# Earlier bank returns, a shift on GpSimd, split token loads and a reordered list in the first layer of a cross-attention kernel

## The chip, the cores and the metric

The kernel runs on one core of a Trainium2 chip. Its time is the device time in microseconds of one execution, given as the median of several runs. Everything is in fp32. The core has five engines, each with its own queue of instructions, taken in order: TensorE (PE in the profile, its weight loads PEld), VectorE (DVE), ScalarE (ACT), GpSimd (POOL) and SyncE (SP, which here only issues DMAs). Matmul results land in PSUM, eight banks of 128 partitions by 512 fp32 values. SBUF holds everything else.

## The reference, cut to what matters

Two layers on 2048 tokens of width 256, with a context of 1601 rows of width 192.

```python
# first layer: tokens route over the context and a gated unit takes the result
tok    = context @ W_proj + b_proj                      # 1601 x 256
attn   = softmax(x @ tok.T / 16)                        # 2048 x 1601
routed = attn @ tok
ps_n, in_n = ln(x, g_state, beta_state), ln(routed, g_input, beta_input)
u = sigmoid([ps_n, in_n] @ W_u + b_u)
r = sigmoid([ps_n, in_n] @ W_r + b_r)
cand = tanh([r * ps_n, in_n] @ W_n + b_n)
x = ln((1 - u) * x + u * cand, g_out, beta_out)
# second layer: 16 heads of 16
h = ln(x, ln1); x = x + mha(h, h, sa_*)
h = ln(x, ln2); x = x + mha(h, context, ca_*)
h = ln(x, ln3); x = x + gelu(h @ mlp_w1.T + mlp_b1) @ mlp_w2.T + mlp_b2
```

The kernel never forms `tok` for the context. It multiplies the tokens by W_proj's transpose first (`queries`), takes scores against the raw context, averages the raw context with the softmax weights (`mean_context`), and projects that mean (`project`).

## The kernel before, in words

Tokens are cut into 16 tiles of 128 (index t) and four blocks of 512 (index b). The program traces operations one after another. A helper `kept` pins an operation behind the one traced before it on the same engine, so that for all compute the engine's order is the traced order. DMAs are not pinned; the framework places them in a queue by its own estimate. The framework sets every semaphore from the order of accesses to each tile.

**First layer, attention** (up to about 206 us). PSUM is a pool, `halves`, of four tiles of two banks, handed out in turn; a tile is given again when all work on its last use is done.
- SyncE issues the loads in traced order: W_proj, the first 512 tokens transposed (`load_xT(0)`, L113 to L115), the context (L121, L123), then bias rows, tokens and further transposed tokens (L224 to L230).
- `queries(b)` (L253) multiplies a block of transposed tokens by the weights, in place in `xy_sb`; ScalarE copies both banks back (L265).
- `query_bias(t)` (L276): GpSimd multiplies a tile of tokens with b_proj (L279) and ScalarE sums it into `cbs`.
- `scores(t)` (L282): TensorE takes scores of a tile against 1601 context rows in two passes (128 features, then 64) into two `half` tiles. VectorE takes the two maxima (L302), and then two operations on one column, on VectorE as well, make the shift (L306 to L310): the smaller of the two negated maxima less the bias, then plus the bias and over 16. ScalarE takes two exponentials with that shift (L313), which frees the two tiles. `turned(t)` (L320) is VectorE's 32x32 block transpose of the result.
- `turn_context` and `spread_context` lay the context out in 32-row pieces by TensorE transposes and 20 DMAs.
- `mean_context(h)` (L361), for each half h of the tokens: four `half` tiles at once; a first pass fills the first bank of each (128 features), a second pass the second bank (64 features). Then eight evictions (L388), c = 0 four times, then c = 1, ScalarE for six and VectorE for two, into `xy_sb`.
- `project(t4)` (L397): four tiles of tokens into one `half`. `project_end(t4)` (L406): for each of the four, VectorE scales by the softmax denominator and adds b_proj out of PSUM into `routed` (L410), then takes the mean and variance (`norm_stats`, L170 and L171).
- `begin_in(b)` (L421) takes the inverse roots of four tiles' variances: two small VectorE operations each, then twelve GpSimd operations on 4 columns (L185 to L188), once for `routed` and once for x, and a VectorE operation that waits for the first. `normed_tile` normalizes x on VectorE, `routed_tile` normalizes `routed` on ScalarE.

The first token half runs `mean_context(0)` and then scores of tiles 8 to 15; after these come `project` 0 and 1, their `project_end` with `begin_in`, `mean_context(1)`, `project` 2 and 3 and their `project_end`. Then `halves` is closed, and a pool `ps_all` of eight one-bank tiles (`bank`) takes its place.

**The list FIRST** (about 206 to 400 us). One list of names, written out by hand (L1093 on), sets the order of the gated unit and of the second layer's preparation. A name calls a step with its arguments: `bi` begin_in, `nx` normed_x (four tiles), `nr` normed_r (four tiles on ScalarE), `ti` a turn of four tiles of normalized x or routed by TensorE with a ScalarE eviction, `r` a reset gate (TensorE, ScalarE's sigmoid, VectorE's product into `rp_T`), `u` and `c` update gate and candidate (TensorE, VectorE's bias add, ScalarE's function), `b` the blend and its statistics (VectorE), `ro` and `rs` inverse roots (GpSimd), `no` and `ns` normalizations, `ts` turns for self attention, `k`, `v`, `q`, `qs` keys, values, queries and their spreading by SyncE's DMAs (L576), `ck`, `cv`, `cs` the same for cross attention (`cs` issues from ScalarE's queue), `REL` gives first-layer memory back and starts the second context load, `cw` loads cross attention's weights, and `L` is one lead unit: four score matmuls and four VectorE maxima (L660), work that the main loop would otherwise do. There are 19 of them. Around the list's start, the second layer's buffers are made: 16 DMAs by SyncE (`ones_beside`, L545), eight DMAs that load `sa_wo` (`load_wo`, L527, issued by GpSimd), eight for `bias8` (L564) and three rows of zeros for the query buffers (L642).

**The main loop** (400 us to the end) goes over 464 units of scores, exponentials and values, less 19 done ahead, with the projections and norms hung in between; then the MLP. The change doesn't touch it.

Of the kernel before, what the change touches and what calls it, by code (L numbers as in the profile page):

```python
# [10 lines left out]
ALU = mybir.AluOpType  # L11
# [3 lines left out]
P = 128  # L15
S = 2048
D = 256
L = 1601
# [3 lines left out]
HD = 16  # L22
HP = 32
# [4 lines left out]
QB = 512  # L28
# [42 lines left out]
def xattn_kernel(  # L71
# [9 lines left out]
    nc = tc.nc  # L81
# [11 lines left out]
    def kept(ins):  # L93
        tc.keep_in_program_order(ins)
        return ins
# [14 lines left out]

    xy_sb = pa.tile([P, 2, S], F32, name="xy_sb")

    def load_xT(b):  # L113
        at_b = slice(b * QB, (b + 1) * QB)
# [86 lines left out]
    T8 = NT // 2  # L201
# [32 lines left out]
    def half():  # L234
        return halves.tile([P, 2, QB], F32, name="half")
# [14 lines left out]
    kept(nc.scalar.copy(wT_sb[:, :, P:], pt[:, :, P : 2 * P]))  # L250


    def queries(b):  # L253
        pt = half()
        for m in range(2):
            for c in range(2):
                mm(
                    pt[:, m, :],
                    wT_sb[:, c, m * P : (m + 1) * P],
                    xy_sb[:, c, b * QB : (b + 1) * QB],  # L260
                    start=(c == 0),
                    stop=(c == 1),
                )
        for m in range(2):
            kept(nc.scalar.copy(xy_sb[:, m, b * QB : (b + 1) * QB], pt[:, m, :]))  # L265

# [94 lines left out]
    def mean_context(h):  # L361


        accs = [half() for _ in range(4)]

        def part(dst, i, kb, feats, **kw):
            r = slice(i * HP, (i + 1) * HP)
            mm(
                dst[:, : T8 * HP].rearrange("p (t a) -> p t a", a=HP),
                ctx4[r, kb, feats],  # L370
                pT[r, :, kb * HP : (kb + 1) * HP],
                skip_group_check=True,
                **kw,
            )

        for kb in range(KB):
            for i, acc in enumerate(accs):
                part(acc[:, 0, :], i, kb, slice(0, P), start=(kb == 0), stop=(kb == KB - 1))
        for kb in range(KB):
# [3 lines left out]
        uT = xy_sb[:, :, h * T8 * P : (h + 1) * T8 * P].rearrange("p c (t i a) -> p c t i a", i=4, a=HP)  # L383
        for c in range(2):
            for i, acc in enumerate(accs):
                copy = nc.vector.tensor_copy if (i % 2 and c) else nc.scalar.copy
                kept(
                    copy(  # L388
                        uT[:, c, :, i, :],
                        acc[:, c, : T8 * HP].rearrange("p (t a) -> p t a", a=HP),  # L390
                    )
                )
        ts = slice(h * T8, (h + 1) * T8)
        kept(nc.vector.tensor_add(rdens[:, ts], dens[:, ts, 0], dens[:, ts, 1]))
        kept(nc.vector.reciprocal(rdens[:, ts], rdens[:, ts]))
# [7 lines left out]
                mm(pt[:, i, :], xy_sb[:, c, tok], w, start=(c == 0), stop=(c == 1))  # L403
        return pt

    def project_end(t4, pt):  # L406
        for i in range(4):
            t = 4 * t4 + i
            kept(
                nc.vector.scalar_tensor_tensor(  # L410
                    routed[:, t, :], pt[:, i, :], rdens[:, t : t + 1], row("b_proj"),
                    ALU.mult, ALU.add,
                )
            )
            norm_stats(mv_r, routed[:, t, :], t)

# [31 lines left out]
    xns.update({2: xns[0], 3: xns[1]})  # L448


    queries(0)
    query_bias(0)
    scores(0)
    turn_context(0, 4)
# [50 lines left out]
    for t4, pt in got:  # L505
        project_end(t4, pt)
    l0.close()


# [7 lines left out]
    def heads(ap, w):  # L517
        return ap.rearrange("p (h w) -> p h w", w=w)

    def load_wo(pool, w, name):  # L520

        t = pool.tile([P, G // 2, D], F32, name=name)
        v = w.rearrange("(pr hf j w) n -> hf j w pr n", hf=2, j=4, w=HP)
        for hf in range(2):
            for j in range(4):
                r = j * HP + hf * HD
                nc.gpsimd.dma_start(t[r : r + HD, :, :], v[hf, j, :HD])  # L527
        return t

    ps_all = ctx.enter_context(tc.tile_pool(name="ps_all", bufs=8, space=PSUM))  # L530
# [369 lines left out]
    def normed_x(b):  # L900
        for i in range(4):
            normed_tile(xns[b][i], 4 * b + i)

    def normed_r(b):
        for t in range(4 * b, 4 * b + 4):
            routed_tile(t)
# [143 lines left out]
    ca = {}  # L1050
# [14 lines left out]
    def load_ca_weights():  # L1065
        wqs["ca"] = load_compact(
            ca["pool"], ca_wq, P, "ca_wq_sb", nc.gpsimd, ca["stage"].tile([P, 4 * D], F32, name="stage")
        )
        wos["ca"] = load_wo(ca["pool"], ca_wo, "ca_wo_sb")

    def k_ca_block(pr, n):
        n0, nw = even_blocks(L, 4)[n]
# [2 lines left out]
    def k_ca_spread(pr):  # L1075
# [6 lines left out]


    STEPS = {
        "bi": begin_in, "nx": normed_x, "nr": normed_r, "ti": turned_in, "r": reset, "u": update,
        "c": candidate, "b": blend, "ro": root_out, "no": normed_out, "rs": root_sa,
        "ns": normed_sa, "ts": turned_sa, "k": k_sa_block,
        "v": lambda b, i: v_block("sa", sa_wv_sb, hT_sa, 4 * b + i),
# [2 lines left out]
        "cs": k_ca_spread, "cv": lambda i: v_block("ca", ca_wv_sb, ca["ctx"], i), "L": lead_unit,  # L1091
    }
    FIRST = (  # L1093
# [9 lines left out]
    ).split()  # L1103
    for w in FIRST:
        name = w.rstrip("0123456789.")
# [157 lines left out]
```

## Time and profile before

| what | us |
| --- | --- |
| median of three runs | 1945.0 (1943.71 to 1945.75) |
| the profiled execution | 1942.26 |
| its span | 1940.5 |
| TensorE busy | 1908.6 |
| VectorE busy | 1430.3 |
| ScalarE busy | 1334.4 |
| GpSimd busy | 671.8 |
| granted TensorE clock, mean | 0.993 |
| last first-layer token tile evicted from PSUM (L410) | 205.95 |
| end of the list FIRST | about 400 |

The profile is of one execution; its own time is beside its span, and 2.7 us under the median. An engine's busy time counts its instructions and not its waits. In a row of the timeline the first two numbers are the start and the length, `x` is how many instructions were merged, and the brackets tell how long the engine stood before it and what ended that. `SPq` and `ACTq` are the issuing of DMAs.

### The profile page before, as it was taken

Reading aid. Unit: us, or ns where it says so; the run is one execution under the profiler, and the core shown is the slowest. Engines: PE = TensorE matmul, PEld = TensorE weight load, DVE = VectorE, ACT = ScalarE, POOL = GpSimd, SP = SyncE. Lnnn points to the kernel's source line nnn. Section 1 sums busy time; section 2 is a strip of 40 time slices with the busy share of each in tenths; the row PEclk is TensorE's granted clock in tenths of the full one; section 3 lists DMA queues with packets and bytes.
Section 4 is the critical chain, followed back from the end, with each engine's and each line's share of the span. In section 5 each row is a group of like instructions: output and inputs, shape, how many; then the busy total and the mean of one; then the engine's idle time right before and its main releaser. Section 6 shows DMA issues by size and latency. Waiting matters only on the chain.

```text
span 1940.5 us, 39176 instructions
## 1 busy us (share of the span) xinstructions
PE 1908.6 (98%) x14774; PEld 852.7 (44%) x14774; DVE 1430.3 (74%) x2554; ACT 1334.4 (69%) x2590; POOL 671.8 (35%) x850
## 2 busy tenths in 40 slices
PE   9997999999999999999999999999999999999999
PEld 4756675533333333433333334333333433443366
DVE  4472476788888888888888888788888878886210
ACT  3230423268887888788878887887888788888621
POOL 1201424124443444344444444343544343443010
PEclk9998998999999999999999999999999999999999
DMA  8310403600000000000000000000000000000000
GB/s 212 99 33 2 51 1 70 81 12 5 5 5 5 5 5 5 5 5 8 5 5 5 5 5 5 5 5 4 26 27 5 7 6 5 5 5 2 1 22 22
DMA packets 32766, 38.27 MB, mean 20 GB/s; under 512 B 12416, under 2 KB 24832, under 8 KB 32192
## 3 DMA queue, kind: packets, MB, share of 16 engines
q1 hardware_dynamic: 30496, 29.72, 7.3%
q0 software_dynamic: 1424, 4.38, 0.8%
q10 hardware_dynamic: 656, 1.67, 0.6%
q8 instruction: 116, 1.90, 0.4%
q14 instruction: 74, 0.61, 0.1%
HBM read 16.27 MB, written 2.62 MB: 10 GB/s over the span
## 4 chain that ended last, share of the span: by engine, by line
PE 82%; DVE 5%; POOL 1%; DMA 1%; issue 0%; SPq 0%; ACT 0%; ACTq 0%; DVEq 0%
PE bank L98 81%; DVE mxp L660 2%; PE bank L101 1%; DMA k_sa<-k 1%; DVE bn_st L882 0%; SPq L576 0%; DVE res L964 0%; DVE cand_sb L963 0%; DVE res L981 0%; DVE cand_sb L946 0%; DVE bn_st L817 0%; DVE cand_sb L962 0%; PE half L98 0%; DVE res L976 0%; DVE routed L410 0%
## 5 line engine op out<-in xcount | busy, mean ns | idle before, releaser
L660 DVE TENSOR_REDUCE mxp<-bank 128x1 f32<-128x512 f32 x1792 | 1109.9, 682 | 172.9 <-PE bank L98 166.5
L706 ACT ACTIVATE pt<-bank 128x512 f32<-128x512 f32 (+1 forms) x1856 | 959.6, 603 | 201.6 <-PE bank L98 201.1
L732 POOL TENSOR_TENSOR acc<-acc,part 128x512 f32<-128x512 f32 x414 | 524.7, 1267 | 838.2 <-ACT part L731 838.2
L98 PE MATMUL bank<-qa,k_sa 32*128 32x512 f32 x2048 | 519.9, 615 | 0.4
L98 PE MATMUL bank<-k_sa,qa 32*128 32x512 f32 x2048 | 506.2, 618 | 4.6 <-ACT k L1018 2.6
L98 PE MATMUL bank<-k_ca,qa 32*128 32x512 f32 (+1 forms) x2048 | 432.4, 531 | 0.0
L98 PE MATMUL bank<-qa,k_ca 32*128 32x512 f32 (+1 forms) x1664 | 414.6, 617 | 0.0
L98 PEld LDWEIGHTS bank<-qa,k_sa 32*128 32x128 f32 x2048 | 216.4, 183 | 226.9 <-DVE mxp L660 203.6
L98 PE MATMUL bank<-pt,v_sa 128*32 128x512 f32 x2048 | 272.8, 605 | 0.0
L731 ACT COPY part<-bank 128x512 f32<-128x512 f32 x414 | 253.5, 612 | 13.0 <-PE bank L98 11.1
L98 PEld LDWEIGHTS bank<-qa,k_ca 32*128 32x128 f32 (+1 forms) x1664 | 166.2, 179 | 179.6 <-DVE mxp L660 143.4
L98 PEld LDWEIGHTS bank<-k_sa,qa 32*128 32x128 f32 x2048 | 198.3, 183 | 74.1 <-ACT pt L706 43.9
L98 PE MATMUL bank<-pt,v_ca 128*32 128x512 f32 (+1 forms) x1664 | 224.9, 605 | 0.0
L98 PEld LDWEIGHTS bank<-k_ca,qa 32*128 32x128 f32 x2048 | 196.5, 184 | 47.3 <-ACT pt L706 32.6
L98 PEld LDWEIGHTS bank<-pt,v_sa 128*32 128x32 f32 x2048 | 40.3, 108 | 192.0 <-ACT pt L706 191.0
L98 PEld LDWEIGHTS bank<-pt,v_ca 128*32 128x32 f32 (+1 forms) x1664 | 34.6, 108 | 150.6 <-ACT pt L706 148.5
L98 PE MATMUL half<-l_pT,ctx 32*128 32x256 f32 (+1 forms) x1632 | 73.0, 385 | 11.4 <-DVE routed L410 9.1
L1181 DVE TENSOR_TENSOR o<-bank,res 128x512 f32<-128x512 f32 (+1 forms) x9 | 5.6, 631 | 97.0 <-PE bank L98 97.0
L98 PE MATMUL half<-ctx_w,xy_sb 128*128 128x512 f32 (+5 forms) x256 | 71.1, 516 | 1.9 <-DVE xy_sb L388 1.2
L98 PEld LDWEIGHTS half<-l_pT,ctx 32*128 32x128 f32 (+1 forms) x1632 | 62.6, 163 | 21.9 <-DVE routed L410 10.0
L313 ACT ACTIVATE pr_xn<-half,l_nmx 128x801 f32<-128x801 f32 (+1 forms) x32 | 29.4, 925 | 44.2 <-DVE l_nmx L310 44.2
L98 PE MATMUL bank<-hT_sa,k_sa 128*128 128x512 f32 x128 | 55.7, 593 | 0.0
(186 smaller groups left out, 1277.4 us busy)
## 6 DMA issues: line engine op xcount, KB each, us to landing
ctx<-l_pT SPq DMA_DIRECT2D x8, 312.0 KB
ctx<-l_pT SPq DMA_DIRECT2D x8, 288.0 KB
xy_sb<-in_xT_dram SPq DMA_DIRECT2D x4, 512.0 KB
res<-in_x_dram SPq DMA_DIRECT2D x4, 512.0 KB
k_sa<-hT_sa SPq DMA_DIRECT2D x16, 128.0 KB
k_sa<-k SPq DMA_DIRECT2D x64, 32.0 KB
qa<-hT_sa SPq DMA_DIRECT2D x64, 32.0 KB
qa<-hT SPq DMA_DIRECT2D x64, 32.0 KB
```

What stands on the lines that cost most here:

```text
L98: kept(nc.tensor.matmul(out_, lhsT, rhs, **kw))
L101: kept(nc.tensor.transpose(out_, in_, ident))
L313: nc.scalar.activation(pr_xn[:, t % 2, k0 : k0 + kw], pieces[i], AF.Exp, bias=nmx, scale=1.0 / 16.0, accum_out=dens[:, t, i : i + 1],)
L660: kept(nc.vector.tensor_reduce(mxps[n][:, j, qt, kb : kb + 1], mx, AX.X, ALU.max))
L706: kept(nc.scalar.activation(pt[:kw], sc[:kw], AF.Exp, scale=HD**-0.5))
L731: kept(nc.scalar.copy(part, av))
L732: kept(nc.gpsimd.tensor_add(accs[n], accs[n], part))
L1181: kept(nc.vector.tensor_add(o[:, some, :], po[:, :n, :], res[:, t0 : t0 + n, :]))
```

## The change

Five things, all ahead of the main loop.

1. The tokens of block 0 are loaded in two halves: 256 before the context, 256 after the bias row and the first token load. `queries` takes a start and a width; the second half of block 0 is multiplied right before block 1.
2. The two small operations of the shift move from VectorE to GpSimd. The first becomes a `tensor_scalar` with two scalar columns.
3. In `mean_context` the four c = 0 evictions, on ScalarE, move between the two passes; c = 1 alternates ScalarE and VectorE.
4. `project_end` no longer takes statistics. For the first `on_scalar` of its four tiles, ScalarE scales out of PSUM and GpSimd adds b_proj; the others stay on VectorE. The statistics of tiles 0 to 7 follow both project_ends, those of tiles 8 to 15 become a step `st` of the list. `routed_tile` takes tiles 0 to 7 ahead of `mean_context(1)`, so `nr1` leaves the list.
5. The list FIRST has a new order, and `sa_wo` is loaded by SyncE's queue.

```diff
-    load_xT(0)
+    load_xT(0, 0, QB // 2)
...
     load_x(0)
+    load_xT(0, QB // 2, QB // 2)
     load_xT(1)
...
         kept(
-            nc.vector.scalar_tensor_tensor(
+            nc.gpsimd.tensor_scalar(
                 nmx, nm2[:, 0:1], nm2[:, 1:2], cb, ALU.min, ALU.subtract
             )
         )
-        kept(nc.vector.tensor_scalar(nmx, nmx, cb, 1.0 / 16.0, ALU.add, ALU.mult))
+        kept(nc.gpsimd.tensor_scalar(nmx, nmx, cb, 1.0 / 16.0, ALU.add, ALU.mult))
...
+        for i in range(4):
+            evict(0, i, nc.scalar.copy)
         for kb in range(KB):
             c = slice(kb % 2 * (C - P), (kb % 2 + 1) * (C - P))
             for i, acc in enumerate(accs):
                 part(acc[c, 1, :], i, kb, slice(P, C), start=(kb < 2), stop=(kb >= KB - 2))
...
+        for i in range(4):
+            evict(1, i, (nc.scalar.copy, nc.vector.tensor_copy)[i % 2])
...
-    def project_end(t4, pt):
+    def project_end(t4, pt, on_scalar):
         for i in range(4):
             t = 4 * t4 + i
-            kept(
-                nc.vector.scalar_tensor_tensor(
-                    routed[:, t, :], pt[:, i, :], rdens[:, t : t + 1], row("b_proj"),
-                    ALU.mult, ALU.add,
-                )
-            )
-            norm_stats(mv_r, routed[:, t, :], t)
+            if i < on_scalar:
+                kept(nc.scalar.mul(routed[:, t, :], pt[:, i, :], rdens[:, t : t + 1]))
+                kept(nc.gpsimd.tensor_add(routed[:, t, :], routed[:, t, :], row("b_proj")))
+            else:
+                kept(
+                    nc.vector.scalar_tensor_tensor(
+                        routed[:, t, :], pt[:, i, :], rdens[:, t : t + 1], row("b_proj"),
+                        ALU.mult, ALU.add,
+                    )
+                )
...
+    queries(0, QB // 2, QB // 2)
     queries(1)
...
     for t4 in range(2):
-        project_end(t4, got[t4])
-        begin_in(t4)
+        project_end(t4, got[t4], (4, 2)[t4])
+    for t in range(T8):
+        norm_stats(mv_r, routed[:, t, :], t)
+    for b in range(2):
+        begin_in(b)
     for b in range(2):
         for i in range(4):
             normed_tile(xns[b][i], 4 * b + i)
-    for t in range(4):
+    for t in range(T8):
         routed_tile(t)
     mean_context(1)
     got = [(t4, project(t4)) for t4 in range(2, 4)]
     for t4, pt in got:
-        project_end(t4, pt)
+        project_end(t4, pt, 2 * (t4 - 2))
...
-    wos["sa"] = load_wo(sa_pool, sa_wo, "sa_wo_sb")
+    wos["sa"] = load_wo(sa_pool, sa_wo, "sa_wo_sb", nc.sync)
...
-        "ti0.2 ti0.3 ti0.0 ti0.1 ti1.0 nr1 ti1.1 u0.0 r0.0 bi2 r0.1 u0.1 nx2 c0.0 bi3 ti1.2 "
-        "b0.0 ti1.3 nr2 c0.1 b0.1 nr3 ro0 r1.0 ti2.0 r1.1 no0.0 ti2.1 u1.0 no0.1 no0.2 no0.3 ti2.2 "
-        "rs0 ti2.3 c1.0 b1.0 c1.1 nx3 r2.0 u1.1 b1.1 r2.1 ro1 ti3.0 ti3.2 ns0 u2.0 c2.0 no1.0 "
-        "ti3.1 no1.1 b2.0 no1.2 ti3.3 u2.1 c2.1 b2.1 ro2 no1.3 ts0.0 r3.0 r3.1 no2.0 u3.0 rs1 "
-        "c3.0 no2.1 ts0.1 c3.1 ns1 b3.0 u3.1 b3.1 k0.0 v0.0 k0.1 ro3 v0.1 v0.2 v0.3 ts1.0 REL "
-        "no2.2 ts1.1 no2.3 q0 rs2 no3.0 no3.1 k1.0 ck1.0 cv0 ns2 v1.0 ck0.0 v1.1 k1.1 no3.2 L "
-        "no3.3 ts2.0 cw ts2.1 cv1 cv2 v1.2 L k2.0 v1.3 L ck0.1 rs3 q1 cv3 cv4 L ck1.1 cv5 cv6 ns3 "
-        "L cv7 L ck1.2 cv8 cv9 L ck0.2 ts3.0 L v2.0 v2.1 ts3.1 v2.2 L k3.0 L ck1.3 L ck0.3 L cs0 "
-        "cv10 v2.3 v3.0 cs1 L cv11 qs1 v3.1 v3.2 L k2.1 L k3.1 v3.3 L L q2 L L q3 cv12"
+        "st3 st2 bi3 ti0.2 ti0.3 ti0.0 ti0.1 ti1.0 ti1.2 ti1.3 ti1.1 r0.0 r0.1 bi2 u0.0 nr3 u0.1 "
+        "c0.0 b0.0 nx3 c0.1 nx2 b0.1 r1.0 ro0 nr2 r1.1 u1.0 no0.0 no0.1 c1.0 u1.1 b1.0 ti2.2 "
+        "no0.2 ti2.0 ti2.3 ti2.1 ti3.0 c1.1 b1.1 ro1 no0.3 r2.0 r2.1 rs0 ti3.2 ns0 no1.0 u2.0 "
+        "no1.1 c2.0 u2.1 ti3.1 ti3.3 b2.0 ts0.0 c2.1 no1.2 ts0.1 b2.1 ro2 r3.0 no1.3 r3.1 rs1 "
+        "no2.0 u3.0 c3.0 v0.0 ns1 b3.0 c3.1 u3.1 b3.1 k0.0 v0.1 no2.1 ts1.0 ts1.1 REL v0.2 v0.3 "
+        "ro3 no2.2 v1.0 k0.1 no2.3 v1.1 v1.2 q0 no3.0 no3.1 k1.0 no3.2 cv0 rs2 ck0.0 cv1 ck0.1 "
+        "v1.3 k1.1 L cv2 no3.3 cv3 ns2 L rs3 ck0.2 ts2.0 ck1.0 ts2.1 q1 ns3 v2.0 cw L k2.0 L "
+        "v2.1 ck1.1 L cv4 ts3.0 v2.2 L cv5 v2.3 ts3.1 L ck1.2 L k3.0 L cv6 L ck0.3 ck1.3 L v3.0 "
+        "L k3.1 v3.1 L cv7 cv8 cv9 L cv10 cv11 cs1 v3.2 L qs1 k2.1 v3.3 L cs0 L q2 L L q3 cv12"
```

More of the change, by code (lines that the diff above doesn't have):

```diff
@@ L111, in xattn_kernel, with load_xT @@
     xy_sb = pa.tile([P, 2, S], F32, name="xy_sb")
-    def load_xT(b):
-        at_b = slice(b * QB, (b + 1) * QB)
+    def load_xT(b, n0=0, nw=QB):
+        at_b = slice(b * QB + n0, b * QB + n0 + nw)
         nc.sync.dma_start(xy_sb[:, :, at_b], xT.rearrange("(c p) n -> p c n", p=P)[:, :, at_b])
-    load_xT(0)
+    load_xT(0, 0, QB // 2)
     ctx_w = p0.tile([P, 2 * L], F32, name="ctx_w")
@@ L250, in xattn_kernel, with queries @@
     kept(nc.scalar.copy(wT_sb[:, :, P:], pt[:, :, P : 2 * P]))
-    def queries(b):
+    def queries(b, n0=0, nw=QB):
         pt = half()
+        at_b = slice(b * QB + n0, b * QB + n0 + nw)
         for m in range(2):
@@ L257, in queries @@
                 mm(
-                    pt[:, m, :],
+                    pt[:, m, :nw],
                     wT_sb[:, c, m * P : (m + 1) * P],
-                    xy_sb[:, c, b * QB : (b + 1) * QB],
+                    xy_sb[:, c, at_b],
                     start=(c == 0),
@@ L264, in queries @@
         for m in range(2):
-            kept(nc.scalar.copy(xy_sb[:, m, b * QB : (b + 1) * QB], pt[:, m, :]))
+            kept(nc.scalar.copy(xy_sb[:, m, at_b], pt[:, m, :nw]))
     H0 = (L + 1) // 2
@@ L378, in mean_context, with evict @@
                 part(acc[:, 0, :], i, kb, slice(0, P), start=(kb == 0), stop=(kb == KB - 1))
+        uT = xy_sb[:, :, h * T8 * P : (h + 1) * T8 * P].rearrange("p c (t i a) -> p c t i a", i=4, a=HP)
+        def evict(c, i, copy):
+            kept(
+                copy(
+                    uT[:, c, :, i, :],
+                    accs[i][:, c, : T8 * HP].rearrange("p (t a) -> p t a", a=HP),
+                )
+            )
+        for i in range(4):
+            evict(0, i, nc.scalar.copy)
         for kb in range(KB):
@@ L382, in mean_context @@
                 part(acc[c, 1, :], i, kb, slice(P, C), start=(kb < 2), stop=(kb >= KB - 2))
[L383 to L386, printed above, removed]
-                kept(
-                    copy(
-                        uT[:, c, :, i, :],
-                        acc[:, c, : T8 * HP].rearrange("p (t a) -> p t a", a=HP),
-                    )
-                )
+        for i in range(4):
+            evict(1, i, (nc.scalar.copy, nc.vector.tensor_copy)[i % 2])
         ts = slice(h * T8, (h + 1) * T8)
@@ L404, in project @@
         return pt
[L406 removed]
+    def project_end(t4, pt, on_scalar):
         for i in range(4):
             t = 4 * t4 + i
[L409 to L415 removed]
+            if i < on_scalar:
+                kept(nc.scalar.mul(routed[:, t, :], pt[:, i, :], rdens[:, t : t + 1]))
+                kept(nc.gpsimd.tensor_add(routed[:, t, :], routed[:, t, :], row("b_proj")))
+            else:
+                kept(
+                    nc.vector.scalar_tensor_tensor(
+                        routed[:, t, :], pt[:, i, :], rdens[:, t : t + 1], row("b_proj"),
+                        ALU.mult, ALU.add,
+                    )
+                )
     rins = {}
@@ L448, in xattn_kernel @@
     xns.update({2: xns[0], 3: xns[1]})
-    queries(0)
+    queries(0, 0, QB // 2)
     query_bias(0)
@@ L518, in heads, with load_wo @@
         return ap.rearrange("p (h w) -> p h w", w=w)
-    def load_wo(pool, w, name):
+    def load_wo(pool, w, name, queue):
         t = pool.tile([P, G // 2, D], F32, name=name)
@@ L526, in load_wo @@
                 r = j * HP + hf * HD
-                nc.gpsimd.dma_start(t[r : r + HD, :, :], v[hf, j, :HD])
+                queue.dma_start(t[r : r + HD, :, :], v[hf, j, :HD])
         return t
@@ L902, in normed_x, with stats_in @@
             normed_tile(xns[b][i], 4 * b + i)
+    def stats_in(b):
+        for t in range(4 * b, 4 * b + 4):
+            norm_stats(mv_r, routed[:, t, :], t)
     def normed_r(b):
@@ L1068, in load_ca_weights @@
         )
-        wos["ca"] = load_wo(ca["pool"], ca_wo, "ca_wo_sb")
+        wos["ca"] = load_wo(ca["pool"], ca_wo, "ca_wo_sb", nc.gpsimd)
     def k_ca_block(pr, n):
@@ L1084, in xattn_kernel @@
     STEPS = {
-        "bi": begin_in, "nx": normed_x, "nr": normed_r, "ti": turned_in, "r": reset, "u": update,
+        "st": stats_in, "bi": begin_in, "nx": normed_x, "nr": normed_r, "ti": turned_in, "r": reset, "u": update,
         "c": candidate, "b": blend, "ro": root_out, "no": normed_out, "rs": root_sa,
```

## The prediction

> **What bounds the kernel now.** I read the page first: busy times and the rows by slice.
>
> ```profile
> PE 1908.6 (98%) x14774; PEld 852.7 (44%) x14774; DVE 1430.3 (74%) x2554; ACT 1334.4 (69%) x2590; POOL 671.8 (35%) x850
> ...
> PE   9997999999999999999999999999999999999999
> ...
> PEclk9998998999999999999999999999999999999999
> ```
>
> TensorE sets the end. It is idle for 1940.5 - 1908.6 = 31.9 us of the span, nearly all of it ahead of 400 us, and the change touches nothing later. So it can win that idle time there, and the time lost to a lower granted clock. Next, the waits of TensorE in the first 420 us (total, times, longest):
>
> ```profile
> PE half L98 <- DVE routed L410: 9.1, 2, 7.3
> PE bank L101 <- DVE routed L410: 4.6, 1, 4.6
> PE bank L98 <- ACT k L1018: 2.6, 1, 2.6
> ...
> PE half L98 <- ACT xy_sb L388: 1.3, 1, 1.3
> PE bank L98 <- POOL rs_sa_a L186: 1.3, 1, 1.3
> ```
>
> Line 410 is `project_end`: 13.7 us of idle, against 2.4 us for the evictions of `mean_context` (L388, by ACT and DVE) and 3.9 us near 322 us. The busy time by stretch gives the clock (start:end, length, busy of PE, PEld, DVE, ACT, POOL, then the clock):
>
> ```profile
> 140.00:150.00 10.00, 7.35 (x34) 5.43 (x32) 8.84 (x21) 1.93 (x4) 0.47 (x3) 0.93 0.35 105
> 150.00:160.00 10.00, 3.58 (x33) 2.98 (x37) 4.71 (x17) 2.07 (x4) 5.98 (x31) 0.50 0.00 1
> 160.00:170.00 10.00, 10.00 (x168) 8.89 (x164) 2.84 (x9) 0.00 (x0) 3.18 (x15) 0.88 0.02 3
> ...
> 320.00:340.00 20.00, 16.58 (x56) 9.41 (x57) 15.62 (x35) 5.37 (x9) 4.94 (x13) 0.74 0.19 42
> ```
>
> A long pause costs twice: the clock is half from 148.68 to 162.33, 206.71 to 210.12 and 322.76 to 333.00 us. Then the timeline around the longest pause, the evictions near 102 us, and SyncE's queue:
>
> ```profile
> 102.07 1.75 ACT L388 COPY xy_sb<-half 128x256 f32<-128x256 f32 x6 [30.86 <-PE half L98]
> 102.75 0.98 DVE L388 COPY xy_sb<-half 128x256 f32<-128x256 f32 x2 [30.48 <-ACT xy_sb L388]
> ...
> 148.25 0.83 PE L98 MATMUL half<-l_pT,ctx 32*128 32x256 f32 x2 [1.73 <-DVE routed L410]
> ...
> 156.42 9.87 PE L98 MATMUL half<-l_pT,ctx 32*128 32x256 f32 x124 [7.34 <-DVE routed L410]
> ```
>
> ```profile
> 304.20 13.12 SPq L576 DMA_DIRECT2D k_sa<-k  x16
> 317.42 2.50 SPq L576 DMA_DIRECT2D qa<-hT_sa  x4
> ```
>
> The second row matters most: VectorE's copy of one bank of a `half` tile started only when ACT's copy of that tile's other bank had ended. Two accesses of one PSUM tile are ordered here, even two reads of different banks.
>
> **The change, part by part.** The sum stands against the profiled execution, 1942.3 us (1.8 around the span), 2.7 below the median of 1945.0.
>
> *Earlier bank returns behind projects 0 and 1.* Now VectorE frees the two tiles: each token tile costs 0.45 (L410) plus statistics, 1.05 us from start to start. The first tile is free at 148.2, the second at 156.4, with begin_in's 3.08 us wait for GpSimd between. After: ACT, free from 142.8, scales project 0's four pieces. The nearest rows are 0.41 (L280) and 0.50 from start to start (L442): four end by 144.8, ahead of project 1's end at 145.9. Two more on ACT end at 146.9. VectorE's two of the same tile queue behind them by the 102.75 row, two at 0.48: 147.9. TensorE resumes at 147.9 for 156.4: -8.5. The matmuls from 156.42 to 162.33 no longer run at half clock: -2.95. A 1.7 us pause may still bring one slow stretch of 3.41 us (1.7 us lost, +0.65 as expected loss). Together -10.8; ends -12.4 (no ordering, full clock) and -9.6 (ACT at the 0.59 us duration of L442 and a slow stretch). The eight statistics (0.53 each), six GpSimd adds (0.72 each), begin_in 0 and 1 and the eight ACT rescalings (0.5 each) lie behind mean_context(1), which takes TensorE 37 us; the longest chain of them, two begin_in of 2 x 6.7 us on GpSimd, ends near 168.
>
> The 0.65 rests on the row at 322.76, where the clock fell behind a 1.25 us pause and before the 2.60 us one. [...]
>
> *The same behind projects 2 and 3.* Now eight pieces at 1.05 us, 198.13 to 206.0, all before a bank of the new pool is given. After: four without statistics (198.1 to 200.1), then when project 3 ends at 201.6 two on ACT and, ordered behind, two on VectorE: 203.5. -2.5 (ends -1.5, -3.5), and half the chance of saving the slow stretch at 206.71 (1.7 us): -0.85.
>
> *Evictions of mean_context, twice.* c=0's four move between the passes, on ACT at 0.265 us from start to start. Pass 2 writes the tiles they read, so by the ordering above TensorE waits about 1.2 us there. At the end four are left, two engines: first buffers free after 0.45 instead of 1.18 and 1.27. Net +0.8 for both (ends -1.6 if pass 2 does not wait, +1.8 if the wait is 1.7). The wait rests on the 102.75 row: this program orders tiles, not banks. [...]
>
> *Shift on GpSimd.* VectorE loses 0.22 + 0.21 us a tile but had idle time waiting for TensorE (0.18 to 0.26 us a tile), so nothing is gained. GpSimd starts 0.08 us behind VectorE and spaces such small operations 0.28 us (L185 to L188), pair ready after 0.57, as now. A tile's buffers come round every two tiles with 1.1 us spare. POOL's adds beside VectorE transposes take 1.27 us, as alone, so turned(t-1) does not hold the pair. Queued behind the pair is the next tile's query_bias product (0.72), needed 2 us later. 0; ends 0 and +5 (held for the whole 1.87 us transpose: 2.4 us latency, 0.4 us a tile over 14 tiles).
>
> *Half the first tokens.* TensorE's idle time here is 1.80 (tokens), 0.67 (copies), 0.88 (buffers). Queries can start when the weights are copied, 6.7 for 7.58, and take 1.72 for 3.44, but the other 1.72 us only moves behind `spread_context`. The context's rows land until 13.55; 256 KB fewer ahead of them, at 300 to 400 GB/s, bring that 0.7 to 0.9 us sooner, and scores' second pass then waits about 1.0. New idle: 0.9 + 0.6 + 1.0 + 0.5 = 3.0 for 3.35: -0.3 (ends -2.0, +1.0). The extra transfer takes one SyncE issue (0.6 us), delaying the later tokens and rows, wanted 20 us later.
>
> *sa_wo by SyncE.* GpSimd loses 4.2 us of issues (L527). SyncE gains eight at 0.42 to 1.25 us: 3 to 10 us behind the k_sa ones, ahead of bias8 and the zero rows. SyncE has nothing from 227.6 until 304, and the first user of qa starts near 320. 0.
>
> *The new order.* Work is the same (24 turns and turned_sa at 0.43, 24 resets, updates and candidates at 3.44, 8 k at 1.72, 16 v and 13 cv at 0.86, 4 q at 3.44, 8 ck at 1.35, 19 lead units at 0.93: 174 us in both), so only stalls count. Early: st3, st2 put 8 x 0.53 = 4.2 us on VectorE, bi3 and bi2 each a 3.1 us wait for GpSimd. TensorE has 8 turns (0.43), two resets and two updates (3.44 each) = 17 us first. Following VectorE's queue, the reset products for c0.0 are ready near 215.5, wanted at 221; those for c1.0 at 237.4, wanted at 238. If that cover goes, TensorE waits. Late: at 320 to 333 TensorE idles 1.25 + 2.60 and loses half of 7.6 us to the clock, 7.65 in all. Two causes: SyncE's 16 k issues of 0.82 us ahead of qa's, and rs2's chain on GpSimd (311.1 to 322.2) behind cw's loads, with ACT waiting in ns2. The new list has 11.2 for 9.5 us of TensorE work from k0.0 through q0, and 8.8 for 3.9 us between rs2 and ns2. I take two thirds: -5 (ends -8.2, which adds the 0.53 at 267 us, and +6, 2 us for a wait of the same kind at each of cs0, qs1 and c1.0).
>
> Sum: -10.8 - 3.35 + 0.8 + 0 - 0.3 + 0 - 5 = -18.6. Against the median: 1945.0 - 18.6 = 1926.4.
>
> **Rivals.**
> *The order gives back.* The pauses at 148 to 156 and 206 close, but the same stalls return before the first lead unit: -18.6 + 5 + about 4 = -10: 1935. For it: rs3 now follows rs2 closely on GpSimd, and qs1 stands only 3.7 us of TensorE work ahead of its user where it had 9.
> *Banks, not tiles.* No eviction waits and the late stall goes whole: -12.4 - 5.2 - 1.6 - 2 - 8.2 = -29 at the most, half of the way -24: 1921. Against it: the row at 102.75.
> *Slower: inverse roots hold VectorE.* VectorE keeps its order, so bi3, bi2, ro0 and ro1 hold all behind them until GpSimd answers, 3.4 us each. At the 11.1 us of rs_sa at 311.1, four chains cost 4 x 7.7 = 31, less about 6 of cover: +25, total +6: 1951. It decides at about 10.5 us a chain. Against: GpSimd has no issues or loads left there.
> *The change is small.* Stalls of 15 to 22 us spread over the order: within 4 us of 1945.
>
> **How the numbers follow.** Forecast (-15 to -22): 0.50. Order gives back (-8 to -15): 0.25. Banks: 0.11. Slower: 0.08. Small: 0.06, of which some 0.05 within 0.2%, about what a measurement can tell here. So faster 0.87, same 0.05, slower 0.08. The range, 1915 to 1940, takes in the first three and leaves out about 0.15.
>
> **What would show it.** Waits of TensorE on routed falling from 13.7 to about 4 us; 150 to 160 at full clock with over 180 matmuls; a new wait of 1.2 us on L388's successor between the passes, twice; first exponentials of tile t no later behind the maxima; 320 to 340 without the half clock. Wrong would make me: a tile period over 4.43 us; TensorE waiting for rp_T or GpSimd's roots between 215 and 260; a wait for qa at the first or the seventeenth lead unit.

## The result, and the profile after

The changed kernel takes 1925.24 us (1923.94 to 1926.08) where the one before took 1944.70 (1943.71 to 1945.75): a ratio of 0.990, 95% interval 0.988 to 0.992, or 19.5 us less. The forecast was 1926.4.

The profiled execution of the changed kernel took 1926.08 us (span 1924.3). Busy times and the rows by slice, from its page:

```profile
PE 1907.7 (99%) x14782; PEld 857.3 (45%) x14782; DVE 1415.6 (74%) x2514; ACT 1340.2 (70%) x2600; POOL 685.6 (36%) x882
...
PE   8999999999999999999999999999999999999999
...
PEclk9999999999999999999999999999999999999999
```

TensorE is idle for 16.6 us where it was for 31.9. Its waits in the first 420 us (total, times, longest):

```profile
PE bank L98 <- DVE v_ca L1049: 2.8, 2, 2.0
PE half L98 <- DMA ctx_w<-in_ctxT_dram: 2.0, 1, 2.0
PE bank L101 <- DVE routed L420: 1.9, 1, 1.9
PE half L98 <- DVE l_pT L240: 1.5, 1, 1.5
PE half L98 <- DVE routed L420: 1.3, 1, 1.3
PE half L98 <- ACT pr_xn L315: 1.2, 1, 1.2
```

The waits on `routed` fell from 13.7 to 3.2 us and those on `mean_context`'s evictions from 2.4 to 0.2 (0.11 each, too short for the list). Two are new: the wait for the context's rows at 10.10, and the first line, on VectorE's additions of the value bias (L1049) near 310 us. The busy time by stretch (start:end, length, busy of PE, PEld, DVE, ACT, POOL, then the clock):

```profile
140.00:150.00 10.00, 8.84 (x45) 6.74 (x42) 6.44 (x7) 5.26 (x14) 4.62 (x8) 1.00 0.51 157
150.00:160.00 10.00, 9.87 (x184) 9.90 (x188) 5.10 (x25) 1.90 (x4) 4.12 (x21) 1.00 0.01 3
...
300.00:320.00 20.00, 17.18 (x57) 8.90 (x56) 11.74 (x30) 4.78 (x9) 9.27 (x30) 0.83 0.28 61
320.00:340.00 20.00, 20.00 (x95) 10.79 (x97) 12.62 (x26) 8.06 (x14) 5.17 (x16) 1.00 0.45 54
```

From 150 to 160 us TensorE runs 184 matmuls for 33, at full clock. The late stall did not go, it moved: half clock (a granted 0.50) from 312.23 to 319.05 for 322.76 to 333.00. And there is half clock where before had none: 18.68 to 22.09 and 28.92 to 32.33.

One point followed through the two profiles says where the time went:

| TensorE reaches | before | after | difference |
|---|---|---|---|
| the first matmul of `mean_context(0)` | 64.86 | 68.97 | +4.1 |
| the first of `project(0)` | 138.7 | 141.0 | +2.3 |
| the first transpose of the list | 206.10 | 194.05 | -12.05 |
| the first values of the main loop | 406.22 | 387.68 | -18.54 |
| the last values | 1819.25 | 1803.08 | -16.2 |

The last 2.4 us are lost in steps of 0.16 to 0.25 us spread over the main loop, with no pause of TensorE over 0.2 us there. From its first to its last values the loop takes 1413.0 to 1413.3 us in ten of the thirteen profiles of this document, and 1415.4, 1414.9 and 1415.6 in the changed kernel, banks_only and two_tiles. In the changed kernel and two_tiles the steps stand at the same places of the loop, which speaks for the program and against chance; but whole_tokens, with the same list and loop, has none. Each kernel has one profile, so what they are stays open. The +4.1 at the start had to be explained: the forecast had -0.3.

### The profile page after: what moved, and what is told of

Same layout as the page of the kernel before. It is cut to its first block, busy times and chain, and to the rows that moved or that the text cites. A ratio compares the mean times of both kernels' runs of the same rounds, so it can differ in the third digit from the quotient of the medians.

```text
span 1924.3 us, 39225 instructions
## 1 busy us (share of the span) xinstructions
PE 1907.7 (99%) x14782; PEld 857.3 (45%) x14782; DVE 1415.6 (74%) x2514; ACT 1340.2 (70%) x2600; POOL 685.6 (36%) x882
## 4 chain that ended last, share of the span: by engine, by line
PE 86%; DVE 2%; DMA 1%; SPq 0%; ACT 0%; issue 0%; POOL 0%; DVEq 0%
PE bank L98 85%; DVE mxp L673 1%; PE bank L101 1%; DMA k_sa<-k 1%; SPq L589 0%; ACT pt L719 0%; DVE bn_st L830 0%; DVE nr_v L178 0%; DVE mvb L831 0%; DVE routed L420 0%; DVE v_ca L1049 0%; ACT k L1035 0%; POOL rs_sa_y L188 0%; POOL rs_sa_a L186 0%; POOL rs_sa_a L185 0%
## 5 line engine op out<-in xcount | busy, mean ns | idle before, releaser
L744 ACT COPY part<-bank 128x512 f32<-128x512 f32 x414 | 252.2, 609 | 13.8 <-PE bank L98 10.4
L304 DVE TENSOR_REDUCE l_nm<-half 128x1 f32<-128x801 f32 (+1 forms) x32 | 30.2, 986 | 42.0 <-PE half L98 42.0
```

The source lines that it names most:

```text
L744: kept(nc.scalar.copy(part, av))
```

## The experiments

Ratios are to the kernel before, run beside each; 0.001 is 1.9 us.

**banks_only**, one part of the change alone: `project_end` with its third argument, the statistics behind it and `routed_tile` for T8 tiles as in the change, and of the list only this:

```diff
-        "ti0.2 ti0.3 ti0.0 ti0.1 ti1.0 nr1 ti1.1 u0.0 ...
+        "st2 st3 ti0.2 ti0.3 ti0.0 ti0.1 ti1.0 ti1.1 u0.0 ...
```

> The kernel before with one part of the change: the scalings behind the projections on ScalarE and VectorE, their statistics behind them, and the old order with the statistics of tiles 8 to 15 put at its head. Theory A (the two terms of the prediction, -10.8 and -3.35): 14 us faster than before, 1930 to 1931; the waits of TensorE on `routed` fall from 13.7 to about 4 us and the clock is full from 146 to 200 us. Theory B (the trace of the changed kernel read as 'TensorE reached the list 12.05 us earlier, with the start 4.1 us later and two pauses of 1.8 us for code gone'): the part alone is worth about 15 us, 1929 to 1930. Theory C (given back: what is late next stalls the same list): 1936 to 1942, with new pauses between 200 and 330 us.

Measured: 1930.87 for 1943.82, ratio 0.9936 [0.9923, 0.9948], -12.4 us. Pauses at 148 and 192 us of 1.29 and 1.93 for 9.07 and 4.55, and full clock from 10 to 310 us. A holds in its mechanism; -14.15 lies inside the interval (-15.0 to -10.1). What was won by 206 us stands at the main loop: no give-back.

**evict_only** and **shift_only**, two more parts alone, each shown in part:

```diff
+        for i in range(4):
+            evict(0, i, nc.scalar.copy)
         for kb in range(KB):
             c = slice(kb % 2 * (C - P), (kb % 2 + 1) * (C - P))
...
```

```diff
-            nc.vector.scalar_tensor_tensor(
+            nc.gpsimd.tensor_scalar(
                 nmx, nm2[:, 0:1], nm2[:, 1:2], cb, ALU.min, ALU.subtract
...
```

> The kernel before with one part of the change: c=0 of `mean_context` evicted between the two passes. Theory A (the prediction: tiles are ordered and the second pass waits for it, +0.8): 1945.5, and the second pass runs at full pace only some 1.2 us after the first has ended, twice. Theory B (banks, no wait): -1.6 to -2.4, 1942.3 to 1943.1, the second pass at full pace at once. Theory C (tiles are ordered, but the wait is 0.5 to 0.8 us each time, because the four tiles are given back one by one while TensorE goes on in those it has, against 1.06 and 1.17 us won at the end): about -0.9, 1943.8.

> The kernel before with one part of the change: a tile's shift made by GpSimd. Theory A (the prediction, 0): no difference, 1943.8 within 1.5 us, and the period of a tile between 105 and 138 us stays 4.43 to 4.44 us, because TensorE sets it. Theory B (GpSimd answers later, or is held by VectorE's transposes; the prediction's upper end): 0.4 us a tile over 14 tiles, +5, and TensorE shows waits on pieces of scores there.

Measured: evict_only 1943.45 for 1943.82, ratio 0.9999 [0.9990, 1.0008]; the interval cannot part A from C, the trace can. From the last matmul start of the first pass to that of the twenty-first of the second it is 0.81 us in every execution without the part and 1.56 to 1.59 in every one with it: a wait of 0.77 us a pass, that no pause shows, because the matmuls of the tiles already given back run in it: those of the four tiles first start 0.45, 0.72, 1.00 and 1.27 us behind the first pass, as the copies end one by one. The copies read one bank and the matmuls write the other, so the order goes by tile here. From the timeline of the changed kernel:

```profile
70.21 30.02 PE L98 MATMUL half<-l_pT,ctx 32*128 32x256 f32 x648 [0.53 <-ACT xy_sb L267]
92.13 1.20 ACT L385 COPY xy_sb<-half 128x256 f32<-128x256 f32 x4 [16.78 <-PE half L98]
105.12 0.65 ACT L385 COPY xy_sb<-half 128x256 f32<-128x256 f32 x2 [11.79 <-PE half L98]
105.23 0.76 DVE L385 COPY xy_sb<-half 128x256 f32<-128x256 f32 x2 [28.51 <-PE half L98]
105.55 4.95 PE L98 MATMUL half<-ctx_w,xy_sb 128*128 128x289 f32 x17
```

The four copies stand in the middle of the 648 matmuls, with no idle time beside PE's group. Behind the second pass the two engines copy out of different tiles, and there they do run side by side (105.12 and 105.23); at the kernel before's 102.75 VectorE waited for ScalarE's copy of the same tile. The pauses of 1.18 and 1.27 us at the end become 0.11 each in the changed kernel. Net 2 x 0.77 - 1.07 - 1.16 = -0.7: theory C.

shift_only 1944.92 for 1944.88, ratio 1.0004 [0.9995, 1.0012]: no difference, theory A. The maxima of a tile start every 4.43 or 4.44 us as before; the exponential starts 0.3 us later behind them (0.93 for 0.62), and nothing waits for it.

**whole_tokens**, the changed kernel with that part undone:

```diff
-    load_xT(0, 0, QB // 2)
+    load_xT(0)
...
-    load_xT(0, QB // 2, QB // 2)
...
-    queries(0, 0, QB // 2)
+    queries(0)
...
-    queries(0, QB // 2, QB // 2)
```

> The changed kernel with one part undone: the first block's tokens are loaded in one transfer ahead of the context, and its queries made in one go. Theory A (the prediction: the half load is worth -0.3): 1925.5, no difference that can be measured. Theory B (the trace of the changed kernel: it came to the first `mean_context` 4.1 us later than the kernel before, and this is the half load's doing): 3 to 4 us faster than the changed kernel, 1921 to 1922. Theory C (the pauses are as long as before, 5.1 for 4.8 us, and the two stretches of half clock behind them, 3.3 us, fell to that one execution): 1924.5 to 1926, and a profile whose first 70 us hold a stretch of half clock or not, whatever the load.

Measured: 1925.77, ratio 0.9904 [0.9890, 0.9917] for 0.9899: 0.5 us by the medians, A or C. Its profile has half clock at the start as well: the mean clock is 0.91, 0.83 and 0.83 from 10, 20 and 30 us on, each over 10 us. The time of TensorE's arrival at `mean_context(0)`, with its idle time and the length at half clock by then, in the executions profiled (counted from the first record of the clock at 4.9 to 6.7 us, in banks_only at 10.4):

| load | arrival | idle | half clock |
|---|---|---|---|
| whole: before, banks_only, evict_only, shift_only, whole_tokens | 64.9, 66.2, 69.2, 70.9, 70.6 | 4.8, 4.5, 5.5, 5.8, 5.7 | 0, 0, 6.8, 10.2, 10.2 |
| half: after, old_order, ca_loads, two_tiles, both, old_loads, both_again | 69.0, 67.7, 67.3, 69.5, 68.9, 68.8, 66.0 | 5.1, 5.0, 4.6, 6.0, 5.7, 5.1, 3.6 | 6.8, 3.4, 3.4, 6.8, 6.8, 6.8, 3.4 |

The means are 68.4 and 68.2. The profiled execution of the kernel before had the earliest arrival of the five with the whole load; the +4.1 is a draw of the start and not the change.

**old_order**, the changed kernel without the new order:

```diff
-        "st3 st2 bi3 ti0.2 ti0.3 ti0.0 ti0.1 ti1.0 ti1.2 ...
+        "st2 st3 ti0.2 ti0.3 ti0.0 ti0.1 ti1.0 ti1.1 u0.0 ...
```

> The changed kernel with one part undone: the old order of the list, with the statistics of tiles 8 to 15 put at its head, as the part on the banks needs them. Theory A (the prediction: the new order is worth -5): 1930. Theory B (the two traces: pauses of 5.15 us become 2.81 and half clock costs 3.4 for 5.1, so -4): 1929, with the pauses of TensorE near 310 to 320 us back on k_sa's rows, 1.3 and 2.6 us. Theory C (the order is worth nothing, the pauses move whatever it is): 1924 to 1926.

Measured: 1929.52, ratio 0.9926 [0.9914, 0.9939] for 0.9899: the order is worth 4.3 us by the medians, 5.2 by the ratios. The two intervals, [0.9882, 0.9916] and [0.9914, 0.9939], just touch, so the size is known to some 4 us only. The pauses near 310 us are back, 1.86 and 2.59 us, with 10.24 us of half clock.

**ca_loads**, to find what is left of that stall. The 16 used of each head's 32 columns of ca_wq go straight to their place:

```diff
-        wqs["ca"] = load_compact(
-            ca["pool"], ca_wq, P, "ca_wq_sb", nc.gpsimd, ca["stage"].tile([P, 4 * D], F32, name="stage")
-        )
-        wos["ca"] = load_wo(ca["pool"], ca_wo, "ca_wo_sb", nc.gpsimd)
+        wqs["ca"] = ca["pool"].tile([P, 2, D], F32, name="ca_wq_sb")
+        for c in range(2):
+            nc.scalar.dma_start(
+                wqs["ca"][:, c, :].rearrange("p (h w) -> p h w", w=HD),
+                ca_wq[c * P : (c + 1) * P].rearrange("p (h w) -> p h w", w=HP)[:, :, :HD],
+            )
+        wos["ca"] = load_wo(ca["pool"], ca_wo, "ca_wo_sb", nc.scalar)
```

> The changed kernel, with the loads of ca_wq and ca_wo taken off GpSimd: ScalarE issues them, and ca_wq lands compacted, so that GpSimd copies nothing. Theory A: the pauses left at 309 and 313 us (0.82 + 1.99) and the half clock behind them (6.83 us, 3.4 lost) come from the chain of twelve GpSimd operations of ro3, which took 11.4 us (292.93 to 304.32) with five issues of ca_wo (0.51 to 0.56 each) and a wait of 4.18 us for ca_wq's rows inside it, where the chain at 309.53 took 3.3. VectorE stood behind it for 6.96 us. Without the loads it takes 3.3 to 3.5 us, both pauses and the half clock go: -5 to -6, 1919 to 1920.5. Theory B (VectorE has too much to do there in any case, or rs2's own chain of 3.3 us is what it lacks): the chain shortens, the pauses stay above 1.5 us in sum, 1923 to 1926. Theory C: ScalarE's issues (0.5 to 0.6 each) hold its evictions of k, and TensorE waits for those: slower than 1926.

Measured: 1916.85, ratio 0.9856 [0.9843, 0.9870]: 8.4 us below the changed kernel by the medians, more than A's 5 to 6, and A holds in its mechanism. First the changed kernel's timeline, GpSimd's chain of ro3 from its first operation to its last and who stood behind it:

```profile
292.93 0.36 POOL L185 TENSOR_TENSOR rs_o_a<-rs_o_y 128x4 f32<-128x4 f32 x1 [2.65 <-DVE rs_o_y L180]
...
299.57 0.40 POOL L160 COPY ca_wq_sb<-stage 128x256 f32<-128x256 f32 x1 [4.18 <-DMA stage<-in_ca_wq_dram]
...
300.56 0.51 POOL L540 DMA_DIRECT2D ca_wo_sb<-in_ca_wo_dram  x1
...
304.12 0.20 POOL L188 TENSOR_TENSOR rs_o_y<-rs_o_y,rs_o_a 128x4 f32<-128x4 f32 x1
304.35 0.49 DVE L998 SCALAR_TENSOR_TENSOR res<-res,rs_o_y,rows_sb 128x256 f32<-128x256 f32 x1 [6.96 <-POOL rs_o_y L188]
309.23 1.12 PE L98 MATMUL bank<-k_sa,qa 32*128 32x512 f32 x2 [0.82 <-DVE v_ca L1049]
312.85 0.16 DVE L901 SCALAR_TENSOR_TENSOR ms_sa<-mv_sa,rs_sa_y 128x4 f32<-128x4 f32 x1 [3.40 <-POOL rs_sa_y L188]
313.40 2.07 PE L98 MATMUL bank<-ca_wv_sb,ctx_sb 96*128 96x256 f32 x4 [1.99 <-DVE v_ca L1049]
```

The list has the loads of ca_wq and ca_wo far behind ro3, but GpSimd meets them inside ro3's chain: it waits 4.18 us for rows of ca_wq that it is to copy, and issues eight DMAs of ca_wo (the expectation counted five), 0.51 to 0.56 us each. The chain takes 11.4 us, VectorE stands for 6.96 of them, then for 3.40 of the next chain, and the bank that TensorE wants is read late. With the loads on ScalarE, the same chain and the stretch behind it:

```profile
293.15 0.36 POOL L185 TENSOR_TENSOR rs_o_a<-rs_o_y 128x4 f32<-128x4 f32 x1 [3.35 <-DVE rs_o_y L180]
...
297.13 0.20 POOL L188 TENSOR_TENSOR rs_o_y<-rs_o_y,rs_o_a 128x4 f32<-128x4 f32 x1
```

```profile
300.00:320.00 20.00, 20.00 (x82) 11.40 (x80) 10.88 (x29) 9.69 (x17) 7.55 (x28) 1.00 0.25 56
```

4.2 us for 11.4, and TensorE busy for all of the 20 us at full clock. That is 6.2 us (0.82 + 1.99 + 3.4); the other 2.2 of the 8.4 agree with the main loop, which takes 1413.2 us here for the changed kernel's 1415.4. Since whole_tokens has GpSimd's loads and a loop of 1413.1, those 2.2 us are not shown to be the loads' doing. The same loads stood in the same chain in the kernel before, from 307.00 to 318.83 us:

```profile
307.00 0.20 POOL L185 TENSOR_TENSOR rs_o_a<-rs_o_y 128x4 f32<-128x4 f32 x1 [2.75 <-DVE rs_o_y L180]
...
315.31 0.40 POOL L160 COPY ca_wq_sb<-stage 128x256 f32<-128x256 f32 x1 [3.98 <-DMA stage<-in_ca_wq_dram]
```

**two_tiles** gives projects 1 and 3 two tiles, **both** has that and ca_loads' edit:

```diff
-        pt = half().rearrange("p b (i d) -> p (b i) d", d=D)
+        pts = [half() for _ in range(1 + t4 % 2)]
+        pt = [pts[i // 2 % len(pts)][:, (i // 2) * (2 - len(pts)), i % 2 * D :][:, :D] for i in range(4)]
...
```

> The changed kernel, with the output of projects 1 and 3 in two PSUM tiles each, two pieces in each, so that ScalarE reads one tile while VectorE reads the other. Theory A (tiles are ordered, also for two readers, and the pauses of 1.29 and 1.93 us are two scalings on ScalarE and then two on VectorE): the two engines run side by side, each pause shrinks by 0.8 to 0.9 us, to about 0.45 and 1.1, and a stretch of half clock behind the second (it came in two of four executions) no longer comes: -1.7 without it, -2.4 with its half chance, 1923. Theory B (VectorE waits for ScalarE by another link than the tile): the pauses stay as they are, 1925.

> The two edits of ca_loads and two_tiles together. Theory A of both: -7 to -8, 1917 to 1918.5. If one of the two holds alone, that one's value. If what is won at 190 us is given back in the list: no more than the loads alone, 1919 to 1920.5.

Measured: two_tiles 1926.58, ratio 0.9909 [0.9894, 0.9924]; both 1916.78, 0.9855 [0.9842, 0.9868]. In the trace the pauses come as A says (0.33 and 1.06 for 0.45 and 1.1), but by another way. In the changed kernel ScalarE waits for all of project 1's matmuls, and VectorE's scalings begin when ScalarE's have ended:

```profile
148.24 0.84 ACT L416 ACTIVATE routed<-half,rdens 128x256 f32<-128x256 f32 x2 [1.31 <-PE half L98]
149.11 0.87 DVE L420 SCALAR_TENSOR_TENSOR routed<-half,rdens,l_rows 128x256 f32<-128x256 f32 x2 [1.73 <-ACT routed L416]
150.13 1.15 PE L98 MATMUL half<-l_pT,ctx 32*128 32x256 f32 x16 [1.29 <-DVE routed L420]
```

In two_tiles ScalarE's tile is complete sooner; its last two scalings end at 148.53, while TensorE still makes VectorE's two pieces. VectorE then waits for TensorE alone, and the pause is 0.33 us:

```profile
146.24 2.29 ACT L417 ACTIVATE routed<-half,rdens 128x256 f32<-128x256 f32 x6
149.12 0.88 DVE L421 SCALAR_TENSOR_TENSOR routed<-half,rdens,l_rows 128x256 f32<-128x256 f32 x2 [0.87 <-PE half L98]
150.06 1.15 PE L98 MATMUL half<-l_pT,ctx 32*128 32x256 f32 x16 [0.33 <-DVE routed L421]
```

The two engines do not read at the same time here, at the second place neither (ScalarE ends at 191.21, VectorE begins at 192.09). The second pause fell from 1.93 to 1.06. But the 1.8 us are not seen in the medians: both is 0.07 us below ca_loads, and two_tiles is above the changed kernel. In their profiles the wait for the context at the start was 2.86 and 2.53 us, for 1.95 and 1.51 without the edit; the scatter of the start in the table above is larger than what is sought.

**old_loads** is old_order with the edit of ca_loads, which is not shown again.

> The kernel of old_order (all of the change but the order), with ca_wq and ca_wo loaded by ScalarE as in ca_loads. Theory A (what the new order was worth, 4.3 us, is what it takes from the one stall that GpSimd's loads make near 310 us; without the loads there is nothing left to take): within 1.5 us of ca_loads, 1917 to 1918.5, with no pause over 1 us between 300 and 320 us. Theory B (the order is worth its 4 us in other places): 1920 to 1922, with pauses of TensorE of 3 us and more left between 200 and 385 us.

Measured: 1925.52, ratio 0.9910 [0.9894, 0.9927]; neither theory. The pauses near 310 us are gone, and another has come at 301.68:

```profile
293.24 4.92 ACTq L1085 DMA_DIRECT2D ca_wq_sb<-in_ca_wq_dram  x1
298.21 0.69 ACT L1035 ACTIVATE k<-bank,bias 128x512 f32<-128x512 f32 x1 [6.73 <-DVE bn_st L895]
298.23 2.56 ACTq L540 DMA_DIRECT2D ca_wo_sb<-in_ca_wo_dram  x3
300.85 0.78 ACT L909 ACTIVATE hT_sa<-bank,cols_sb 128x512 f32<-128x512 f32 x1 [1.95 <-issue]
301.68 1.12 PE L98 MATMUL bank<-hT_sa,sa_wk_sb 128*128 128x512 f32 x1 [3.54 <-ACT hT_sa L909]
```

In the old order ScalarE's issues, 4.92 us for the second of ca_wq and 2.56 for three of ca_wo, stand ahead of an eviction that TensorE needs at once (3.54 us, and 1.7 for the half clock behind it). In the new order the same issues (4.81 us for that of ca_wq) delay nobody. With the loads on ScalarE the new order is worth 8.7 us by the medians (1916.85 for 1925.52), with them on GpSimd 4.3: the two edits do not add. So the price of these loads on ScalarE's queue is set by what the order puts behind them; how much the order is worth with no such load in its way was not measured.

**mid_queries**, both with the second half block's queries moved ahead, and **both_again**, both once more:

```diff
     turn_context(0, 4)
+    queries(0, QB // 2, QB // 2)
     turn_context(4, 4)
...
-    queries(0, QB // 2, QB // 2)
     queries(1)
```

> The kernel of both, with the queries of the second half block (8 matmuls, 1.7 us) put between the first two groups of eight transposes of the context, so that no 3.41 us of the start is filled by transposes alone. [...] Theory C (the second half block's tokens land behind 17 us and TensorE waits for them): a pause on the tokens at 17 us, and 1917 to 1919.

> The kernel of both once more, on the chip of the two others, for the comparison: 1916.8 within 1 us. Its profile shows another draw of the start (the wait for the context's rows was 1.5 to 2.9 us in five executions with the half load, and two of these had half clock behind it).

Measured: mid_queries 1914.60, ratio 0.9853 [0.9839, 0.9868]; both_again 1914.96, the same ratio. No difference. Each of the two has one stretch at half clock, from 29.87 and 26.39 us, right behind transposes of the context and a pause of 1.14 and 1.15 us; neither has one behind the first transposes of the context. What brings the half clock at the start was not shown. The tokens were there in time: no pause at 17 us, C falls. both_again is the same program as both and 1.8 us below it by the medians, the same by the ratios (0.9853, 0.9855); it is the ratios that can be compared.

The best of these are 28.7 to 29.0 us faster than the kernel before (1914.6 to 1915.0 for 1943.61), 1.5%; what takes them there beyond the change is the edit of the loads, with the shorter loop that came with it.

## Why the prediction was right, point by point

The forecast case came (-19.5 for -18.6, inside its own -15 to -22), and all terms but the evictions came near their size. That the total came within 1 us is in part luck: the two terms of the bank returns were 1.8 us too good and that of the evictions 1.5 too bad, the measured parts add up to -17 to -19, and each is known to 1 to 4 us only.

- *Earlier bank returns behind projects 0 and 1*, -10.8. Right in mechanism and size. The pauses of 9.07 us became 1.29 (-7.8), and the half clock went (-2.95). Step: "two more on ACT end at 146.9. VectorE's two queue behind them": they do queue, from 149.11 behind ScalarE's end at 149.08, at times 2.2 us later, like all else behind the start. The 0.65 for a slow stretch was not needed: none of the six executions with the pause of 1.29 had one behind it. The row it rests on is not quite as read: at 322.76 the second pause had begun 0.16 us before, so the idle time ahead of it was 1.41 us and not 1.25.
- *The same behind projects 2 and 3*, -3.35. 4.55 became 1.93 (-2.6 for -2.5). The slow stretch behind it did not come here; it came in whole_tokens, old_order and ca_loads, and not in banks_only and old_loads: the half chance was well put. Both terms together: -12.4 measured for -14.15.
- *Evictions of mean_context, twice*, +0.8. Mis-sized, and wrong in sign: -0.7 by the trace, inside the ends. The reading of the 102.75 row was right, the program orders tiles. What failed is "about 1.2 us there": 0.77, because the tiles are given back one by one; and "first buffers free after 0.45": 0.11.
- *Shift on GpSimd*, 0: right, +0.8 measured with an interval of -1.0 to +2.3.
- *Half the first tokens*, -0.3: not refuted, -0.5 by the medians; the two intervals leave some 4 us either way. Step "scores' second pass then waits about 1.0": it was 1.95 ahead of the first, and from none to 2.9 in other executions.
- *sa_wo by SyncE*, 0: not tried alone. In the trace three of its issues stand at 192.19 and five at 212.57, bias8 follows at 216.72, and TensorE waits for none of them.
- *The new order*, -5: -4.3 to -5.2 measured. The size is right, its working only in part. "I take two thirds" of the late stall: it lost 3.85 to 2.81 us of pauses and 5.1 to 3.4 us by the clock, which is 2.7; the rest is the 0.53 at 267 us and the 0.77 at 395 us, which are gone, and the scatter. Of the "two causes" named, ca_loads shows the second, GpSimd's chain behind the loads, while SyncE's 16 issues are the same in ca_loads, with no pause. The step that went wrong is the cover: more TensorE work around ro3 and rs2 does not shorten ro3's chain, which still held the loads (11.8 us before, 11.4 after), and VectorE, behind it, then read TensorE's banks late.
- *Rival "Slower: inverse roots hold VectorE"* falls, and for the four steps that it names the argument against it held: "GpSimd has no issues or loads left there" is so from 186 to 286 us, and the chains of bi3, bi2, ro0 and ro1 took 3.3 to 4.6 us. What the prediction did not carry over is ro3, where the loads of ca_wo and ca_wq are left: 11.4 us, beyond the 10.5 named as the point from which it decides. It came once, and its price is what the change left unwon: 6.2 us by the pauses and the clock, 8.4 by the medians.
- *Rival "Banks, not tiles"* falls with evict_only, where matmuls wait for reads of the other bank of their tile (0.77 us a pass). *"The order gives back"* falls with banks_only and old_order.

Of what was to show it: "first exponentials no later behind the maxima" was wrong by 0.3 us and cost nothing; "320 to 340 without the half clock" is true only because the stall moved to 309.

## What to carry to other kernels

Look whether two engines that read one PSUM tile only queue, as here (VectorE from 149.11 us, behind ScalarE's end at 149.08); with the output spread over two tiles each started when its own pieces were done, and the pause of 1.29 us became 0.33 in the trace. Look for DMA issues, and copies that wait for a DMA, inside the chain of small operations on which another engine stands; here their place in the written order was not their place in the queue, and taking them away was worth 6.2 us, no less than the reordering around them. But see where they go: on ScalarE's queue they cost 5.2 us in one order and nothing in the other. Before a difference at the start of two profiles is explained, look at the same point in other executions of the same code: here it scattered by 4.4 us over three of them (before, banks_only and evict_only, alike up to there).

## What the runs showed of the hardware

In the profiles of the kernel before and of the changed kernel every change of TensorE's granted clock is between 1.00 and 0.50. All pauses of TensorE over 0.8 us in the first 420 us, from the first record of the clock on (5.32 and 5.03 us), and all times at half clock there:

| run | pause, and its start | clock behind it |
|---|---|---|
| before | 1.80 at 5.78; 0.88 at 26.87; 1.49 at 95.45; 1.18 at 102.05 | full |
| before | 1.73 at 146.52, 7.34 at 149.08 | half, 148.68 to 162.33 |
| before | 1.27 at 192.98 | full |
| before | 4.55 at 201.55 | half, 206.71 to 210.12 |
| before | 1.25 at 319.57, 2.60 at 322.60 | half, 322.76 to 333.00 |
| after | 1.95 at 8.15 | full |
| after | none over 0.8 | half, 18.68 to 22.09 |
| after | 1.15 at 27.30 | half, 28.92 to 32.33 |
| after | 1.29 at 148.84; 1.93 at 192.12 | full |
| after | 0.82 at 308.40, 1.99 at 311.41 | half, 312.23 to 319.05 |

In the changed kernel the half clock at 18.68 came in a row of transposes (matmuls against the identity, 128 and 64 rows in turn) that TensorE had made since 15.17 without a pause, and that at 28.92 behind such transposes (24.93 to 27.30) and the pause of 1.15. The kernel before has the same transposes from 16.37 to 20.06 and from 24.50 to 26.87, the second group with a pause of 0.88 behind it, and full clock to 148.68. The pause of 1.93 us at 192 us cost 1.7 us more in whole_tokens, old_order and ca_loads, which had half clock behind it, and nothing in the changed kernel. So the length of a pause alone does not tell what the clock does behind it, and what else decides was not shown.
